# Shorter pauses in a hand-woven instruction order, and weights that are loaded in four blocks of partitions

## The chip, the cores and the metric

The kernel runs on one core of one Trainium2 chip. The metric is the device time in microseconds (us) of one execution; lower is better. A core has five engines that each work through their own instructions in order and meet only through semaphores: TensorE (PE), VectorE (DVE), ScalarE (ACT), GpSimd (POOL) and SyncE (SP), which here only issues transfers.

## What is computed

The input is x, 16 images of 32 channels of 128 x 128 float32. Four layers follow each other; each normalises x over pairs of channels, computes something from it, and adds the result to x (in the last layer it is x times something).

```python
x = x + L0(gn(x))   # layer 0: a row-wise LSTM along the diagonals, 128 steps
x = x + L1(gn(x))   # layer 1: quantised 3x3 "adder" convolution, -sum |patch - w|
x = x + L2(gn(x))   # layer 2: Hartley transform, 32 x 32 modes mixed, transform back
x = x + L3(gn(x))   # layer 3: five edge operators, normalised over a group of images,
                    #   conv1, pool, conv2, pool, conv3, pool, conv4,
                    #   then three times (deconv 2x2, conv 3x3); times the layer's input
```

Layer 3 normalises each edge operator over an image, so its statistics need a whole image before its first convolution can begin. Layers 2 and 3 treat the images in four groups of four; a group needs layer 1 finished for its own four images and nothing of the other groups.

## The kernel before

**Stages.** `stage0` computes layer 0. `rest` computes the other three. Layer 1 is the class `Differences`: for each image and each half of it (64 rows) it makes 72 arrays of 128 x 8192 float16, max(q - w, 0), one for each tap and block of four output channels, and TensorE adds them up over the input channels. An array (a "tap step" below) is made either by VectorE (line 758, tile `d_dve`, three buffers) or by ScalarE (line 755, tile `d_act`, two buffers); 16 matmuls (line 645) add up one of them. Layers 2 and 3 are the class `After`; for one group `g` it runs in this order:

| step | lines | what it does |
|---|---|---|
| `forward` | 1028-1156 | loads x (`xh`, 1050), transforms columns (1116), turns (1131), transforms rows (1088), stores the modes (1098) |
| `modes`, `add` | 1158-1186 | reads the modes back in two orders (`xs`, `xw`, 1168), combines them on VectorE (1175, 1182) |
| `mixing` | 1193-1228 | mixes channels mode by mode (1203), weights `mix` by 1 MB loads (1190), stores `z` |
| `back` | 1230-1333 | transforms back (1267, 1312), adds to x on VectorE and stores (`take_out`, 1290-1296), new statistics |
| `statistics` | 1376-1488 | Gram matrices of the image rows on TensorE (1403), then the five operators' statistics on VectorE (1463) from tables `gm` |
| `first_layers` | 1504-1542 | folds the operators into conv1's weights (1530, 1532) from tables `v` that GpSimd loads (1517), then conv1 |
| `conv1` | 1662-1775 | borders (1693), then 25 taps of 16 matmuls for each of 8 chunks of 16 rows (1721), pooled and spread into `y1` (1645, 1656, 1659) |
| `small_layers` | 1544-1630 | conv2 to conv4 (1568), two upsamplings (902, 927), weights by `replicated` (819) |
| `last` | 1777-1868 | the third upsampling (902), times x (1850, 1813, 1823), result stored |

**What sets the order.** The order on every engine is decided when the program is built. `Differences.run` writes out its own tap steps and, between two of them, calls `weave.advance`, which puts in as much of `After.work` (a generator) as a small planner finds room for. The planner (`Weave`) keeps an estimated time for each engine: 2.36 us for a tap step on VectorE, 7.15 us on ScalarE, 1 us for its sums on TensorE. The generator yields a positive number after it has emitted that much TensorE work, and a negative one for a pause: `yield -4.0` means that the generator gives nothing more until 4 us have passed on the planner's clock. A pause is no instruction. It only decides how many tap steps, or how many instructions of another group, are emitted ahead of the next instruction, so that this one finds its data when its engine comes to it. `weave.later(24.0, step)` does the same for a single deferred step. Leftover time in which TensorE would be idle during layer 1 is filled with matmuls by zero (`keep_busy`, line 675).

Groups 0 to 2 are woven into layer 1 in this way. What is left of them when layer 1 ends, and group 3, whose images are finished only then, are emitted by `drain`: it takes in turn from the two generators whichever stands earlier on its own planner clock, with all pauses multiplied by 1.5, and by 1 once one of the two is exhausted. Below, "layer 1" is the stretch up to the last tap step, and "the tail" is what comes after it.

**Loads.** SP issues nearly all transfers, in program order. `by_rows` issues one transfer for each block of 32 partitions:

```python
def by_rows(nc, tile, dram, store=False):
    for j in range(4):
        part = tile[32 * j : 32 * j + 32]
        rows = bass.AP(dram.tensor, dram.offset + j * dram.ap[0][0], [list(v) for v in dram.ap[1:]])
```

`replicated` loads small convolution weights four times over, once for each block of 32 partitions, by a single transfer whose source has an outermost dimension of four with step zero. It is called 19 times: seven times in `prepare`, and once for conv2 and twice for conv3 and conv4 in each of the four groups.

Of the kernel before, what the change touches and what calls it, by code (L numbers as in the profile page):

```python
# [815 lines left out]
def replicated(nc, pool, src, n, name):  # L816

    wr = pool.tile([128, n, 32], F32, name=name)
    nc.sync.dma_start(wr, bass.AP(src.tensor, src.offset, [[0, 4], [n * 32, 32], [1, n * 32]]))
    return wr  # L820


# [133 lines left out]
class After:  # L956
# [71 lines left out]
    def forward(self, g):  # L1028

        nc, tc, cst, d, weave = self.nc, self.tc, self.cst, self.d, self.weave  # L1030
        x2, xm_d, z_d = d["x2"], d["xm"], d["z"]
        ahead = self.buffers["t_x"]
        with self.pool("t_m") as mp:
# [9 lines left out]
            with self.pool("t_t") as tp, ExitStack() as rows:  # L1043
# [21 lines left out]
                p = self.acc()  # L1065
# [83 lines left out]
                rows.close()  # L1149
                wp = rows.enter_context(self.pool("t_w", self.buffers["t_w"]))  # L1150
                wt = [self.weights(wp, i) for i in range(self.buffers["t_w"])]
                yield -36.0
                for n in range(8):
                    while steps[n]:
                        weave.done(steps[n])
# [2 lines left out]
    def modes(self, g, b, pool, xs, steps):  # L1158

        nc, weave, xm_d = self.nc, self.weave, self.d["xm"]  # L1160
        xw = pool.tile([128, 16, 32], F32, name="xw", bufs=self.buffers["xw"])
        first = xm_d.offset + (4 * g + b) * 32768
        for half in range(2):
            part = slice(64 * half, 64 * half + 64)
            for dst, at in ((xs[part, 4 * half + b], 512 * half), (xw[part], 512 - 512 * half)):
                rows = bass.AP(xm_d.tensor, first + at, [[1024, 32], [1, 512]])
                for r in range(2):
                    nc.sync.dma_start(dst[32 * r : 32 * r + 32].rearrange("p k y -> p (k y)"), rows)

        def add():  # L1170
            for half in range(2):
                part = slice(64 * half, 64 * half + 64)
                x, sign = xs[part, 4 * half + b], self.cst["sign"][part]

                nc.vector.tensor_copy(xw[part, 0, :], x[:, 0, :])
                for dst, neg in (
                    (x[:, 1:, 1:], xw[part, :0:-1, :0:-1]),
                    (x[:, 1:, 0], xw[part, :0:-1, 0]),
                    (x[:, 0, 1:], xw[part, 0, :0:-1]),
                    (x[:, 0, 0:1], xw[part, 0, 0:1]),  # L1180
                ):
                    nc.vector.scalar_tensor_tensor(dst, neg, sign, dst, ALU.mult, ALU.add)
            weave.dve += 2.4
            steps[2 * b + 1] = None

        steps[2 * b + 1] = weave.later(24.0, add)

    def weights(self, pool, i):
        w = pool.tile([128, 4, 16, C], F32, name="mix")
# [3 lines left out]
    def mixing(self, g, xs, wp, wt):  # L1193


        nc, weave, z_d = self.nc, self.weave, self.d["z"]
        zp = [self.acc() for _ in range(2)]
        zv = [z.rearrange("p (y k b) -> p y k b", k=4, b=8) for z in zp]
        for ky in range(M1):
            w = wt[ky // 4]  # L1200
            for k in [4 * j + i for i in range(4) for j in range(4)]:
                j = k // 4
                nc.tensor.matmul(  # L1203
                    zv[ky // 16][32 * j : 32 * j + 32, ky % 16, k % 4, :],
                    w[:, ky % 4, k, :],
                    xs[:, :, k, ky],
                    start=True,
                    stop=True,
                )
            if ky % 4 == 3 and len(wt) < M1 // 4:  # L1210
                wt.append(self.weights(wp, len(wt)))
            yield 1.0
            if ky % 4 == 3 and 8 < ky < M1 - 1 and not weave.draining:
                yield -5.0
        yield SUMMED
        zs = wp.tile([128, 2, 4, 4, 32], F32, name="zs", bufs=1)
        for half in range(2):
            for y in range(2):
                dst = zs[:, half, :, :, 16 * y : 16 * y + 16].rearrange("p b k y -> p y k b")
                nc.vector.tensor_copy(dst, zv[y][:, :, :, 4 * half : 4 * half + 4])  # L1220
        weave.dve += 2.0
        yield -2.5
        for half in range(2):
            for j in range(4):
                first = z_d.offset + 4 * g * 32768 + 512 * half + 128 * j
                dst = bass.AP(z_d.tensor, first, [[1024, 32], [32768, 4], [1, 128]])
                nc.sync.dma_start(dst, zs[32 * j : 32 * j + 32, half].rearrange("p b k y -> p b (k y)"))
        yield -4.0

    def back(self, g, load):  # L1230

# [5 lines left out]
        with self.pool("t_z") as zp_, self.pool("t_r", ahead) as rp:  # L1237
# [68 lines left out]
            for n in range(16):  # L1306
                s, half = n // 2, n % 2
                pf = [self.acc() for _ in range(2)]
                for i in range(4):
                    for r in range(2):  # L1310
                        part = slice(64 * half + 32 * r, 64 * half + 32 * r + 32)
                        nc.tensor.matmul(  # L1312
                            pf[r][:, W * i : W * i + W],
                            o1[part, 4 * s + i].rearrange("p b o -> p (b o)"),
                            cst["cas_t"][part, :],
                            start=True,
                            stop=True,
                        )
                yield 0.8
                if previous:  # L1320
                    yield -4.5
                    take_out(*previous)
                previous = n, pf
            yield SUMMED
# [51 lines left out]
    def statistics(self, g, pool, frames, sides, out, tables):  # L1376
# [14 lines left out]
            nc.gpsimd.dma_start(gm[k], self.a["gram"][:, k])  # L1391
        f = pool.tile([128, 24], F32, name="es_f")
        ends = (slice(2, 4), slice(W, W + 2))
        yield -14.0
        gram = [self.acc() for _ in range(4)]

        def products(xp, l, rows, width, at, start, stop):
# [51 lines left out]
                ready[ch + ahead, half] = weave.later(2.0, following)  # L1449
            yield -1.0  # L1450
        tables()
        yield -3.0

        for k, s in enumerate((1, 0, 3, 2)):
            nc.vector.tensor_reduce(f[:, 4 + k : 5 + k], sides[:, 2 : H + 2, s], AX.X, ALU.add)
# [4 lines left out]
        for k in range(5):  # L1460
            for blk in range(4):
                w = pool.tile([128, GRAM], F32, name="es_w", bufs=1)
                nc.vector.tensor_tensor_reduce(  # L1463
                    w, gram[blk][:, :GRAM], gm[k], 1.0, 0.0, ALU.mult, ALU.add, accum_out=red[:, blk, k : k + 1]
                )
                weave.dve += 0.7
                if blk % 2:
                    yield -1.0
            if len(gm) < 5:
                gm.append(pool.tile([128, GRAM], F32, name="gm", bufs=tables_ahead))  # L1470
                nc.gpsimd.dma_start(gm[-1], self.a["gram"][:, len(gm) - 1])
        yield -2.0
        p = self.acc()
# [30 lines left out]
    def first_layers(self, g, fp, frames, y2):  # L1504
        nc, tc, weave = self.nc, self.tc, self.weave
        sides = fp.tile([128, H + 4, 4], F32, name="sides")
        ops = fp.tile([128, 2, 5], F32, name="ops")
        wf = fp.tile([128, 90, 32], F32, name="wf")
        b1 = fp.tile([128, 4], F32, name="b1")
        with self.pool("e_v", self.buffers["e_v"]) as pool:  # L1510
            v = []

            def table():

                k, half = len(v) // 2, len(v) % 2
                v.append(pool.tile([128, 45, 32], F32, name="v"))
                nc.gpsimd.dma_start(
                    v[-1].rearrange("p t o -> p (t o)"), self.d["fold"][k, :, 1440 * half : 1440 * half + 1440]
                )

            with self.pool("e_s") as es:
                yield from self.statistics(g, es, frames, sides, ops, lambda: [table() for _ in range(self.buffers["e_v"])])
            yield -0.5
            for n in range(10):
                k, half = n // 2, n % 2
                for part, i in (((0, 81 - 45), 0), ((81 - 45, 45), 1)) if half else (((0, 45), 0),):
                    s = ops[:, i, k : k + 1]
                    to, t = wf[:, 45 * half + part[0] : 45 * half + part[1]], v[n][:, part[0] : part[1]]
                    if k == 0:
                        nc.vector.tensor_scalar(to, t, s, None, ALU.mult)  # L1530
                    else:
                        nc.vector.scalar_tensor_tensor(to, t, s, to, ALU.mult, ALU.add)
                    weave.dve += 0.1 + 0.033 * (part[1] - part[0])
                if len(v) < 10:
                    table()
                yield -2.0
        with self.pool("e_y1") as y1p:
            y1 = self.padded(y1p, 64, "y1")
            self.wc = {"conv2": replicated(nc, y1p, self.a["conv2"], 9, "w_conv2")}
            yield from self.conv1(g, y1p, frames, y1, sides, wf, b1)  # L1540
            with self.pool("e_c2") as cp:
                yield from self.small_layers(cp, None, y1, y2)

    def small_layers(self, cp, rp, y1, y2):
# [3 lines left out]
        if not y1:  # L1548
# [2 lines left out]
            up5, up6 = self.up5.loaded(cp), self.up6.loaded(cp)  # L1551
            y3, y4, y5 = (self.padded(cp, n, f"y{i}") for n, i in ((16, 3), (16, 4), (32, 5)))
            self.y6 = y6 = self.padded(rp, 64, "y6")
            yield -12.0

        def conv(src, n, name, evict):
            rows = min(n // 4, 512 // n)
# [45 lines left out]
        def upsampled(src, n, up, dst):  # L1603

            rows = min(n, 512 // n)
            for r in range(0, n, rows):
# [3 lines left out]
                for blk in range(4):  # L1610
# [8 lines left out]
                        up.bias,  # L1619
                        nc.vector if n == 16 or blk % 2 else nc.scalar,  # L1620
                    )
                yield -2.0 if n == 16 else -8.0

        if y1:
            yield from conv(y1, 64, "conv2", pool_into(y2, 64, 1))
# [404 lines left out]
```

## Time and profile before

| | us |
|---|---|
| median of 3 runs | 6794.93 (6793.73 to 6800.52) |
| the profiled execution, its own time | 6791.52 |
| its span, first to last instruction | 6789.7 |
| layer 1, first to last tap step on VectorE | 689 to 5594 |
| the tail | 5592 to 6790 |
| of the tail: TensorE busy | 940.6 |

The profiled execution's time is 1.8 us above its span and 3.4 us below the median. In the profile, a row of a group view gives line, engine, operation, what it writes and reads, its count, the time in which the engine was busy with it, the mean of one, and the idle time of the engine ahead of it with what ended that idle time. A row of the window view gives, for each engine, busy time and number of instructions in a stretch, then TensorE's granted clock, and the busy share and rate of the transfers. Float32 matmuls stand in the profile as two records each, so one conv1 tap of 16 matmuls is 32 records.

When layer 1 ends in this execution, group 2 is in its `statistics`: 5555 to 5685 us. Its conv1 runs from 5773 to 6122 and its `last` from 6302 to 6506. Group 3 starts at the end of layer 1: transforms from 5653, mixing from 5740, back from 5818, statistics from 6053, conv1 from 6253 to 6593, the end at 6790.

### The profile page before, as it was taken

Reading aid. Unit: us, or ns where it says so; the run is one execution under the profiler, and the core shown is the slowest. Engines: PE = TensorE matmul, PEld = TensorE weight load, DVE = VectorE, ACT = ScalarE, POOL = GpSimd, SP = SyncE. Lnnn points to the kernel's source line nnn. Section 1 sums busy time; section 2 is a strip of 40 time slices with the busy share of each in tenths; the row PEclk is TensorE's granted clock in tenths of the full one; section 3 lists DMA queues with packets and bytes.
Section 4 is the critical chain, followed back from the end, with each engine's and each line's share of the span. In section 5 each row is a group of like instructions: output and inputs, shape, how many; then the busy total and the mean of one; then the engine's idle time right before and its main releaser. Section 6 shows DMA issues by size and latency. Waiting matters only on the chain. (4 is left out here: it accounts for less than half of the span.)

```text
span 6789.7 us, 271989 instructions
## 1 busy us (share of the span) xinstructions
PE 5402.1 (80%) x127580; PEld 2816.8 (41%) x127580; DVE 5640.5 (83%) x6946; ACT 5537.1 (82%) x3419; POOL 90.9 (1%) x83
## 2 busy tenths in 40 slices
PE   3697777787777879997877788999877774897896
PEld 3575333333343433333334343333333343454564
DVE  7898999999999999989999999999999993224223
ACT  3898999999999999999999999999999991132222
POOL 0000000000000010000000000000000000000000
PEclk9998999999999989998989899999889996997997
DMA  7553312213343431312353443222264246342414
GB/s 316 201 189 126 77 49 63 60 30 71 80 127 108 113 109 46 85 44 59 86 152 92 145 117 79 56 57 51 61 139 120 66 135 194 99 149 72 92 42 104
DMA packets 381685, 689.12 MB, mean 101 GB/s; under 512 B 68048, under 2 KB 234448, under 8 KB 369680
## 3 DMA queue, kind: packets, MB, share of 16 engines
q1 hardware_dynamic: 373088, 637.30, 34.2%
q0 software_dynamic: 7040, 33.80, 1.5%
q8 instruction: 998, 16.35, 1.0%
q14 instruction: 127, 1.04, 0.1%
q10 hardware_dynamic: 432, 0.64, 0.0%
HBM read 507.28 MB, written 164.32 MB: 99 GB/s over the span
## 5 line engine op out<-in xcount | busy, mean ns | idle before, releaser
L755 ACT ACTIVATE d_act<-q,neg 128x8192 f16<-128x8192 f16 (+1 forms) x622 | 4404.3, 7148 | 138.0 <-PE acc L645 117.2
L758 DVE TENSOR_SCALAR d_dve<-q,qw 128x8192 f16<-128x8192 f16 (+1 forms) x1682 | 3878.9, 2363 | 163.5 <-PE acc L645 143.3
L645 PE MATMUL acc<-d_dve,sel 128*32 128x512 f16 x26912 | 1864.5, 400 | 475.4 <-DVE d_dve L758 412.2
L645 PEld LDWEIGHTS <-sel 128*32 128x32 f16 x36864 | 1014.3, 100 | 2122.4 <-issue 1455.1
L1721 PE MATMUL acc<-xp,wf 32*32 32x512 f32 x25600 | 1040.4, 616 | 57.4 <-issue 53.3
L645 PE MATMUL acc<-d_act,sel 128*32 128x512 f16 x9952 | 716.4, 408 | 329.6 <-ACT d_act L755 310.0
L1721 PEld LDWEIGHTS acc<-xp,wf 32*32 32x32 f32 x25600 | 416.1, 104 | 429.0 <-issue 345.8
L1659 ACT ACTIVATE y<-pooled,b 32x128 f32<-32x128 f32 x488 | 195.1, 400 | 389.1 <-DVE pooled L1645 382.4
L675 PE MATMUL acc<-q,zero 128*32 128x512 f16 x7088 | 509.2, 399 | 0.0
L902 PE MATMUL acc<-y,u_conv 32*32 32x256 f32 (+1 forms) x9728 | 373.8, 472 | 90.8 <-issue 63.7
L221 PE MATMUL pg<-h,wb 64*64 64x20 f32 (+15 forms) x8192 | 340.1, 303 | 61.5 <-DVE h L249 35.3
L235 ACT ACTIVATE gt<-pg,bias 128x20 f32<-128x20 f32 (+15 forms) x1024 | 332.5, 384 | 42.3 <-PE pg L221 40.4
L1362 ACT ACTIVATE xp<-xp,shift,stats 128x1280 f32<-128x1280 f32 (+1 forms) x128 | 182.6, 1434 | 185.8 <-DMA xp<-x_d 170.6
L221 PEld LDWEIGHTS pg<-h,wb 64*64 64x64 f32 x8192 | 250.1, 149 | 136.9 <-DVE h L249 82.5
L675 PEld LDWEIGHTS <-zero 128*32 128x32 f16 x7088 | 214.7, 101 | 195.7 <-issue 40.2
L1850 DVE TENSOR_SCALAR s<-acc,l_ms,l_one 128x512 f32<-128x512 f32 x128 | 102.1, 821 | 202.8 <-PE acc L902 202.8
L902 PEld LDWEIGHTS acc<-y,u_conv 32*32 32x32 f32 x9728 | 177.0, 111 | 216.4 <-issue 164.2
L1823 ACT ACTIVATE xr<-xr,l_ms 128x1024 f32<-128x1024 f32 x64 | 70.0, 1141 | 222.8 <-DVE xr L1813 222.8
L1403 PE MATMUL acc<-xp 32*64 32x204 f32 (+3 forms) x8576 | 238.6, 344 | 16.1 <-issue 15.6
L1403 PEld LDWEIGHTS acc<-xp 32*64 32x64 f32 (+1 forms) x8576 | 168.2, 135 | 108.9 <-issue 100.4
L221 PE MATMUL pg<-xn,wb 64*64 64x2 f32 (+63 forms) x4096 | 184.1, 289 | 28.6 <-issue 18.6
L1568 PE MATMUL acc<-y,w_conv 32*32 32x512 f32 (+2 forms) x4608 | 162.5, 497 | 28.4 <-issue 16.5
(218 smaller groups left out, 3711.9 us busy)
## 6 DMA issues: line engine op xcount, KB each, us to landing
xp<-x_d SPq DMA_DIRECT2D x112, 640.0 KB
q<-q_d SPq DMA_DIRECT2D x128, 536.2 KB
xr<-x_d SPq DMA_DIRECT2D x128, 512.0 KB
x_in<-in_x_dram SPq DMA_DIRECT2D x16, 2048.0 KB
xn<-in_xs_dram SPq DMA_DIRECT2D x64, 512.0 KB
res<-in_x_dram SPq DMA_DIRECT2D x64, 512.0 KB
x_d<-res SPq DMA_DIRECT2D x64, 512.0 KB
xq<-x_d SPq DMA_DIRECT2D x256, 128.0 KB
```

The costliest lines, as they stand in the source:

```text
L221: nc.tensor.matmul(bank[c][q][64 * pair : 64 * pair + 64, :, :width], wb[half, 4 * kind + KIND[q]].rearrange("p b o -> p (b o)"), v[half], ...
L235: nc.scalar.activation(gt[:, q, :, :n], bank[c][q][:, :, :n], AF.Tanh if q == G else AF.Sigmoid, bias=bias[:, KIND[q] : KIND[q] + 1],)
L645: self.nc.tensor.matmul(acc[k][32 * j : 32 * j + 32, :], self.sel16[:, i // 9, :], d[:, row : row + 4, c : c + W], start=first, stop=last,)
L675: self.nc.tensor.matmul(acc[k][32 * j : 32 * j + 32, :], self.zero, q[:, :4, :W], start=False, stop=False)
L755: nc.scalar.activation(dst, src, AF.Relu, bias=self.neg[:, i : i + 1])
L758: nc.vector.tensor_scalar(dst, src, self.qw[:, i : i + 1], 0.0, ALU.subtract, ALU.max)
L902: nc.tensor.matmul(acc[blk][32 * j : 32 * j + 32, o : o + rows * n], t[part, 4 * par + tap, :], src[part, top : top + rows, left : left + ...
L1362: nc.scalar.activation(v, v, AF.Identity, bias=self.shift3, scale=self.stats3[:, 1])
L1403: nc.tensor.matmul(gram[blk][j : j + width, at : at + n], xp[part, l, 2 + j : 2 + j + width], xp[part, rows, j : j + width + 4], start=sta ...
L1568: nc.tensor.matmul(acc[blk][32 * j : 32 * j + 32, : rows * n], wc[name][part, tap, :], src[part, at : at + rows, kw : kw + n], start=tap == 0,
L1659: nc.scalar.activation(d, s, AF.Identity, bias=bj)
L1721: nc.tensor.matmul(acc[blk][32 * j : 32 * j + 32, :], tap_of("all", tap)[rows], xp[rows, 4 * j + kh : 4 * j + kh + 4, kw : kw + W], start= ...
```

## The change

Ten pauses and one deferral of `After` become shorter, and `replicated` loads through `by_rows`, by four transfers in place of one. The tap steps, the planner's costs, the buffers and the arithmetic are as before. Pauses by place: before mixing 36 to 21, before `add` 24 to 14, within mixing 5 to 2.5, after storing `z` 4 to 1.5, before each `take_out` 4.5 to 3.2 (16 a group), before `statistics` 14 to 9, after its loop 3 to 1, between the operators' statistics 1 to 0.4, between folds 2 to 1.2, before conv3 12 to 7, after a round of the second upsampling 8 to 4.5.

```diff
 def replicated(nc, pool, src, n, name):
     wr = pool.tile([128, n, 32], F32, name=name)
-    nc.sync.dma_start(wr, bass.AP(src.tensor, src.offset, [[0, 4], [n * 32, 32], [1, n * 32]]))
+    whole = bass.AP(src.tensor, src.offset, [[0, 4], [n * 32, 32], [1, n * 32]])
+    by_rows(nc, wr.rearrange("p t o -> p (t o)"), whole)
     return wr
...
@@ forward
-                yield -36.0
+                yield -21.0
...
@@ modes
-        steps[2 * b + 1] = weave.later(24.0, add)
+        steps[2 * b + 1] = weave.later(14.0, add)
...
@@ mixing
-                yield -5.0
+                yield -2.5
...
-        yield -4.0
+        yield -1.5
...
@@ back
                 if previous:
-                    yield -4.5
+                    yield -3.2
                     take_out(*previous)
...
@@ statistics
-        yield -14.0
+        yield -9.0
...
         tables()
-        yield -3.0
+        yield -1.0
...
                 if blk % 2:
-                    yield -1.0
+                    yield -0.4
...
@@ first_layers
                     table()
-                yield -2.0
+                yield -1.2
...
@@ small_layers
-            yield -12.0
+            yield -7.0
...
-                yield -2.0 if n == 16 else -8.0
+                yield -2.0 if n == 16 else -4.5
```

## The prediction

> **What bounds the kernel now.** I read the page first, its shares and its forty slices.
>
> ```profile
> PE 5402.1 (80%) x127580; PEld 2816.8 (41%) x127580; DVE 5640.5 (83%) x6946; ACT 5537.1 (82%) x3419; POOL 90.9 (1%) x83
> ...
> PE   3697777787777879997877788999877774897896
> DVE  7898999999999999989999999999999993224223
> ACT  3898999999999999999999999999999991132222
> ```
>
> The shares of 80 to 83% average over two regimes. In slices 5 to 33 VectorE and ScalarE are full and TensorE is not: layer 1. In the last seven slices TensorE is the busy one: the tail. The window view, cut at layer 1's end and at group 3's steps, says how much room each stretch has.
>
> ```profile
> 689.00:5592.00 4903.00, 3998.74 (x85394) 1851.80 (x85394) 4685.09 (x3858) 4753.48 (x1230) 74.12 (x45) 0.93 0.33 85
> 5592.00:5740.00 148.00, 73.71 (x1762) 53.94 (x1754) 68.23 (x222) 27.14 (x43) 5.32 (x11) 0.72 0.74 219
> 5740.00:5818.00 78.00, 58.24 (x2702) 34.96 (x2704) 5.88 (x28) 0.00 (x0) 0.21 (x1) 0.76 0.17 45
> 5818.00:6006.00 188.00, 167.96 (x4942) 95.23 (x4929) 62.19 (x131) 48.45 (x110) 0.00 (x0) 0.98 0.50 149
> 6006.00:6166.00 160.00, 151.73 (x4744) 83.45 (x4713) 30.50 (x133) 61.62 (x127) 6.47 (x14) 0.99 0.38 113
> 6166.00:6253.00 87.00, 57.78 (x1845) 35.42 (x1842) 63.50 (x180) 7.72 (x13) 2.14 (x4) 0.64 0.19 59
> 6253.00:6593.00 340.00, 302.92 (x9573) 204.45 (x9585) 80.98 (x182) 76.20 (x145) 0.21 (x1) 0.95 0.30 69
> 6593.00:6790.00 197.00, 128.25 (x4385) 84.65 (x4353) 82.38 (x168) 48.38 (x80) 0.00 (x0) 0.78 0.43 96
> ```
>
> The columns are stretch, length, then busy time on PE, PEld, DVE, ACT and POOL. In layer 1 (first row) ScalarE is busy 97% and VectorE 96%: what is woven in there costs their time. In the tail TensorE works 941 of 1198 us. The largest hole is the first 148 us, half idle. The group view of the tail shows two of its causes.
>
> ```profile
> L1203 PE MATMUL acc<-xs,mix 128*32 128x8 f32 x1024 | 16.3, 192 | 33.4 <-DVE xs L1182 28.2 <-issue 5.2
> ...
> L1066 PE MATMUL acc<-diag,cw 32*128 32x256 f32 x2 | 1.2, 710 | 15.2 <-DVE diag L1061 15.2
> ```
>
> Group 3's mixing waits 28 us for its modes; before that its scales wait 15 us on a VectorE that is held by group 2's statistics. So the question is how much more of group 2 is done when the tail begins, what that costs in layer 1, and whether the tail gets shorter by it.
>
> **What the skill says.** The Trainium skill, Perfetto Trace Analysis, section Optimization Strategy: where the most-contended engine changes over time, interleaving the regimes may pay. The rows above agree that there are two regimes. DMA: Bandwidth & Descriptors, section Rules for kernel authors: a leading zero-stride dimension of c copies confines a transfer to at most c of the 16 engines. That is the old form of `replicated`; the trace has no landing times for SP's transfers, and nobody is shown waiting for line 819, so it neither agrees nor disagrees. The same page, Anatomy of one DMA: a semaphore wait is served by the issuing sequencer ahead of dispatch, so a transfer that waits holds SP's queue; here SP spent 1075 us in 56 waits at line 338 for `qt`.
>
> **Where the work moves.** The order of both programs' instructions on each engine can be compared. At the last tap step the changed program stands further: 784 of the 1072 instructions of group 2's Gram matrices (line 1403), its 352 border matmuls (1693), 192 matmuls of conv1 (12 of 200 taps), 20 of its operators' statistics pairs (40 records of line 1463) and all 12 of its accumulating folds (1532) have left the tail. Group 2 is about 100 us of the tail's work ahead, from pauses of two and a half groups. Groups 1 and 2 begin `forward` 19 and 59 VectorE tap steps earlier (956 for 975, 1456 for 1515).
>
> **Cost in layer 1.** Means from the group rows. VectorE gains 40 x 0.337 + 12 x 1.215 + 3 x 0.716 + 22 x 0.173 (line 1433) and small ones, in all 42.4 us. ScalarE gains 15 normalisations (1362) of 1.434 and their edges, 28.4 us. The planner also makes 4 tap steps on ScalarE rather than VectorE (1682 to 1678, 622 to 626): -4 x 2.363 and +4 x 7.148. Sum: VectorE +33.0, ScalarE +57.0. Its last tap step ended at 5590, VectorE's at 5594, so layer 1 ends at 5590 + 57 = 5647: +53. TensorE's extra work, 45 us of Gram matrices and 14 of conv1, takes the place of 23 rounds of 16 zero matmuls (24 us) and of idle time. Some of it will hold up sums:
>
> ```profile
> DVE d_dve L758 <- PE acc L645: 143.3, 97, 7.1
> ...
> ACT d_act L755 <- PE acc L645: 117.2, 51, 8.3
> ```
>
> These two waits (us in total, times, longest) grow in proportion to woven work if all goes as before, some 5% of 117, but part of it is paid by zero matmuls: +2. I take +55.
>
> **Cost of the shorter pauses themselves.** A pause is no instruction; if too short, the next instruction waits at the head of an in-order engine with tap steps (DVE) or their sums (PE) behind it.
> - `add`, 24 to 14: in layer 1 it started 10.8 to 24.5 us after the last of its loads was issued, never waiting. 10 us less leaves 0.8 to 14.5. In the tail two of them waited 4.8 us and ran 0.2 and 0.8 us after that issue, so a landing takes little over that. Cost 0 to 4 us per group; I take 0. Mixing, 36 to 21, follows the last `add` anyway.
> - Mixing's weights: a 1 MB load was issued some 30 us before use (5206.6 for 5237.1); 2.5 us less for every four rows of three buffers leaves over 20. Nothing.
> - Folds, 2 to 1.2: before, one or two between tap steps; now three to seven. A table buffer comes back after three folds, and a table lands 6.0 us after its issue on POOL's queue (720 KB). Three folds of 1.2 to 1.7 us and one tap step are about 7, so where seven folds stand together VectorE waits some 3 to 4 us: up to 10 us over three groups. Gram tables: 1.8 us once before, up to 3 a group. VectorE has 24 us less to add than ScalarE, which covers these; without that cover they would cost 15.
> - `take_out`: 16 per group, still mostly two tap steps apart; `xr` was reloaded 24 us ahead. Conv3's weights were issued 23 us ahead, now 18. The rest defer nothing that was late. Nothing.
> - `replicated`: 19 issues of 0.57 us become 76 of 0.42: 21 us more of SP, spread over the program, with nobody waiting; between -1 and +1 us each if on the path. I take 0. Behind them on SP stand the composed weights (issued 6594, used 6636) and the frames; 2 us do not reach either.
>
> **Gain in the tail.** A conv1 tap takes 1.17 us (1897 records in an unbroken 69.4 us of the chain). For each stretch, group 3's own work plus what the changed order puts beside it:
> 1. To mixing (148): Gram matrices give way to 63 taps, 71 us, with 23 of transforms; the last 30 us still wait for the modes. 138.
> 2. Mixing (78): 14 + 50 taps (56) and issue gaps: 77.
> 3. Back (188): 75 taps in place of 112, some conv2: work 132 for 162, with the 26 us of waits as before: 160.
> 4. Statistics (160): 53 + conv2 to conv4 (27) + the third stage's first rounds (19), no conv1: 99, and 20 of waits: 119.
> 5. Tables (87): a chain of transfers and VectorE, 86.
> 6. Conv1 (340): 200 taps, and 624 in place of 1088 matmuls of group 2's last upsampling: 300.
> 7. Alone (197): unchanged; pauses no longer order anything. 197.
>
> Sum 1077 for 1198: -121; I take -120. Check by work: TensorE loses 75 us, VectorE's hold-ups ahead of it (15 + 10 + 8) go, issue gaps lose 15: -123.
>
> **Sum.** +55 - 120 = -65. The profiled execution's 6791.5 becomes 6726.5; the median stood 3.4 above it: 6730.
>
> **Rivals.**
> - *Group 3's chain is the bound.* For it: stretches 1 and 5 have TensorE idle 50 and 34%. If stretches 1 to 5 keep their lengths and only the sixth falls by 40, layer 1's +55 and 15 us of uncovered table waits are paid for a gain of 40: 6795 + 30 = 6825. It decides as soon as the tail gives back less than 70. Against it: stretches 3 and 4 have TensorE at 89 and 95%. Chance 0.13.
> - *TensorE fills every hole.* Work 866, issue gaps 142, and 34 of waits at the end: 1042, -156; with +52 in layer 1, 6690. Against it: the changed order puts only eight taps before the mixing, where 30 us are idle. Chance 0.14.
> - *The lead is lost in waits of layer 1.* Early instructions stall it by 60 us, 20 a group, over my bound: 6795. Chance 0.09.
> - *The change does not do what it says*: excluded by the order, 784 instructions moved.
>
> **Chances.** Forecast 0.64 (6700 to 6780). A measurement of this kernel can tell 0.2% (14 us) from no change. Faster: 0.64 + 0.14 = 0.78; same 0.09; slower 0.13. The range 6680 to 6800 leaves out the first rival and the fast edge of the second.
>
> **What would show it.** The last tap step near 5647; group 3's conv1 of 300 us; the last stretch of 197; table waits on VectorE under 15 us in all. I am wrong if the waits of tap steps for TensorE rise by tens of us, or if group 3's mixing still begins 148 us after layer 1 with its statistics no earlier.

## The result and the profile after

| | before | changed | ratio, 95% interval |
|---|---|---|---|
| median, us | 6797.73 (4 runs) | 6739.66 (4 runs) | 0.9917, 0.9900 to 0.9934 |
| the profiled execution, us | 6791.52 | 6751.99 | |
| its span, us | 6789.7 | 6750.2 | |

The change makes the kernel 58 us faster; 65 were forecast, and 6739.66 lies 10 us above the forecast of 6730 and inside its range. The profiled execution of the changed kernel is the slowest of its four and stands 12 us above their median, that of before 6 below its own: the two profiles differ by 39.5 us, so stretches compared between them understate the gain by some 18.

The page of the changed kernel: the same two regimes, with the change of regime one slice later (column 35 of the forty).

```profile
PE 5402.1 (80%) x127212; PEld 2825.9 (42%) x127212; DVE 5639.1 (84%) x6966; ACT 5552.5 (82%) x3399; POOL 85.9 (1%) x83
...
PE   3798777788777879997877779998787788887795
...
DVE  7898999999999999999999998899999996144223
ACT  3898999999999999999999999999999996122112
```

Its window view, cut at the end of layer 1 and at group 3's steps (columns as in the forecast):

```profile
689.00:5662.00 4973.00, 4066.16 (x87694) 1881.00 (x87686) 4711.68 (x3972) 4800.11 (x1275) 74.50 (x56) 0.92 0.33 87
5662.00:5784.00 122.00, 103.39 (x2383) 48.97 (x2366) 42.06 (x136) 23.21 (x46) 0.00 (x0) 0.93 0.61 176
5784.00:5866.00 82.00, 73.98 (x2624) 42.38 (x2624) 9.44 (x41) 19.56 (x44) 0.21 (x1) 0.92 0.36 99
5866.00:6031.00 165.00, 142.99 (x4149) 84.68 (x4136) 59.79 (x123) 32.27 (x77) 0.21 (x1) 0.90 0.42 127
6031.00:6182.00 151.00, 113.63 (x3609) 78.13 (x3610) 57.34 (x196) 49.41 (x85) 6.24 (x13) 0.84 0.57 150
6182.00:6266.00 84.00, 49.68 (x1924) 32.62 (x1926) 49.37 (x113) 8.05 (x10) 2.13 (x4) 0.59 0.40 102
6266.00:6553.00 287.00, 258.41 (x8224) 197.11 (x8207) 62.68 (x166) 55.45 (x109) 0.21 (x1) 0.96 0.22 51
6553.00:6750.00 197.00, 124.14 (x4386) 80.68 (x4379) 82.61 (x170) 48.35 (x80) 0.00 (x0) 0.77 0.43 96
```

Layer 1 is longer and the tail is shorter. The first row is 70 us longer than before's. Its busy time grew by 27 us on VectorE and 47 on ScalarE; its idle time (length less busy time) grew from 218 to 261 us on VectorE and from 150 to 173 on ScalarE. The tail's first stretch fell from 148 to 122 us, with TensorE now 85% busy in it, and conv1's from 340 to 287. Counted to the end of the last tap step, layer 1 ends at 5658.5 for 5592.0, and began 2.7 us earlier: +69. The tail is 1091.7 us for 1197.7: -106. Layer 1 differs by up to 17 us between the profiles of runs (below) with the same compute order in it: 4903 us before, 4920 in e1 and 4904 in e4; 4972 in the changed kernel and 4962 in e3. The group view of the tail says what became of the two holes:

```profile
L1204 PE MATMUL acc<-xs,mix 128*32 128x8 f32 x1024 | 14.1, 188 | 18.3 <-DVE xs L1183 10.9 <-issue 7.5
...
L1067 PE MATMUL acc<-diag,cw 32*128 32x256 f32 x2 | 0.7, 426 | 0.0
```

The wait for the scales (15.2 us) is gone, that for the modes fell from 28.2 to 10.9. Line numbers from 820 on are one higher than before; those below are of the changed kernel where its lines are shown.

### The profile page after: what moved, and what is told of

The parts are those of the page before. It is cut to its first block, busy times and chain, and to the rows that moved or that the text cites. A ratio compares the mean times of both kernels' runs of the same rounds, so it can differ in the third digit from the quotient of the medians.

```text
span 6750.2 us, 271326 instructions
## 1 busy us (share of the span) xinstructions
PE 5402.1 (80%) x127212; PEld 2825.9 (42%) x127212; DVE 5639.1 (84%) x6966; ACT 5552.5 (82%) x3399; POOL 85.9 (1%) x83
## 4 chain that ended last, share of the span: by engine, by line
PE 21%; issue 14%; DVE 8%; ACT 6%; DMA 2%; SPq 1%; POOL 0%; DVEq 0%; ACTq 0%; POOLq 0%
PE acc L1722 8%; ACT d_act L755 5%; PE acc L645 5%; DVE d_dve L758 4%; PE acc L903 2%; PE acc L1404 1%; PE acc L1569 1%; DVE y L1657 1%; ACT xp L1363 0%; DMA mix<-in_mix_dram 0%; PE acc L928 0%; DMA v<-fold_d 0%; PE acc L1694 0%; DMA xm_d<-xm 0%; PE acc L1313 0%
## 5 line engine op out<-in xcount | busy, mean ns | idle before, releaser
L1722 PE MATMUL acc<-xp,wf 32*32 32x512 f32 x25600 | 1012.0, 623 | 33.0 <-issue 28.3
L1722 PEld LDWEIGHTS acc<-xp,wf 32*32 32x32 f32 x25600 | 431.8, 105 | 387.3 <-issue 307.4
L675 PE MATMUL acc<-q,zero 128*32 128x512 f16 x6720 | 481.9, 399 | 0.0
L903 PE MATMUL acc<-y,u_conv 32*32 32x256 f32 (+1 forms) x9728 | 356.5, 485 | 95.7 <-issue 53.0
L675 PEld LDWEIGHTS <-zero 128*32 128x32 f16 x6720 | 200.2, 101 | 185.6 <-issue 38.3
L1758 DVE TENSOR_TENSOR acc<-acc,cut 128x4 f32<-128x4 f32 x256 | 35.2, 164 | 232.5 <-PE acc L1722 230.1
```

The source lines that it names most:

```text
L675: self.nc.tensor.matmul(acc[k][32 * j : 32 * j + 32, :], self.zero, q[:, :4, :W], start=False, stop=False)
L903: nc.tensor.matmul(acc[blk][32 * j : 32 * j + 32, o : o + rows * n], t[part, 4 * par + tap, :], src[part, top : top + rows, left : left + ...
L1722: nc.tensor.matmul(acc[blk][32 * j : 32 * j + 32, :], tap_of("all", tap)[rows], xp[rows, 4 * j + kh : 4 * j + kh + 4, kw : kw + W], start= ...
```

## The experiments

All times are medians of four runs and more, beside runs of the kernel before on the same chip; the ratio is to those. The theory is that of the forecast, "the lead": the gain is group 2's work that leaves the tail. Its rivals are the loads and the order inside the tail; later runs ask for the price of single pauses.

**e1: the loads alone.** The kernel before, with `replicated` as changed.

```diff
-    nc.sync.dma_start(wr, bass.AP(src.tensor, src.offset, [[0, 4], [n * 32, 32], [1, n * 32]]))
+    whole = bass.AP(src.tensor, src.offset, [[0, 4], [n * 32, 32], [1, n * 32]])
+    by_rows(nc, wr.rearrange("p t o -> p (t o)"), whole)
```

> The kernel before with the four-block weight loads alone, all pauses as before. Lead theory (the gain is work of group 2 that leaves the tail for layer 1): no waiter stood behind these loads, so no change, within 0.2% of before (6784 to 6811). Rival, the loads: if they were what helped, some 6740.

Measured 6791.25, ratio 0.9993 (0.9985 to 1.0001): no difference that can be told. The loads of small weights are not the gain.

**e3 and e4: the short pauses in one regime only.** In e3 they hold while work is woven into layer 1, in e4 only in the tail; every pause of the change is written like this one (e4 with the two numbers exchanged):

```diff
-                yield -21.0
+                yield -36.0 if self.weave.draining else -21.0
```

> The changed kernel with the short pauses only while work is woven into layer 1; in the tail every pause has its old length. Lead theory: the state at the last tap step is that of the changed kernel (784 Gram matmuls and 12 conv1 taps fewer in the tail), so most of the gain stays, 6735 to 6760. Rival, the order in the tail (shorter pauses there interleave groups 2 and 3 better): the lead is paid for and nothing is got back, 6797 or more.

> The changed kernel with the short pauses only in the tail; while work is woven into layer 1 every pause has its old length. Lead theory: layer 1 ends as before and the tail has all of its work; mixing may start 10 to 15 us earlier, so 6780 to 6797. Rival, the order in the tail: the whole gain, about 6740.

Measured: e3 6735.94, ratio 0.9912 (0.9898 to 0.9926), the whole gain; e4 6809.56, ratio 1.0014 (1.0006 to 1.0022), none, and slightly slower than before where a small gain was expected. The gain comes from the pauses inside layer 1. In the tail they bring nothing: e3's tail, with the old pauses, is 1086 us long, the changed kernel's 1092. Without the lead they cost something there: e4's tail is 1216 us long, for 1198 before and 1200 in e1.

**e5: the same pauses without the lead.** One pause of 200 us before group 0 uses the lead up again.

```diff
-                yield -8.0
+                yield -200.0 if g == 0 else -8.0
```

> The changed kernel, all pauses short, but with one pause of 200 us before group 0, so that the lead is gone: 1824 Gram matmuls are left in the tail, for 1856 before and 1072 in the changed kernel. Lead theory: layer 1 is as short as before, the tail as long: 6780 to 6800. Rival, the order in the tail, or denser weaving as such: about 6740.

Measured 6867.6, ratio 1.0100 (1.0087 to 1.0113). The gain is gone, as the lead theory says, but the kernel is 70 us slower than before, which no theory had. Its tail is 1213 us, 16 more than before and like e4's 1216. Its layer 1 is 4962 us for 4903, although VectorE and ScalarE do almost the same work in it (4682 for 4685 us, 4757 for 4753): the 59 us are waiting. So the short pauses have a price of their own in layer 1, or the shifted start has; the next runs look for its place.

**e7: part of the pauses.** Only the four around the mixing stay short; all others are as before.

```diff
-                    yield -3.2
+                    yield -4.5
...
-        yield -9.0
+        yield -14.0
...
-        yield -1.0
+        yield -3.0
...
-                    yield -0.4
+                    yield -1.0
...
-                yield -1.2
+                yield -2.0
...
-            yield -7.0
+            yield -12.0
...
-                yield -2.0 if n == 16 else -4.5
+                yield -2.0 if n == 16 else -8.0
```

> The changed kernel with short pauses only around the mixing (before it, before its combining step, within it, after storing its result); all others as before. Its tail has 1328 Gram matmuls left, for 1856 before and 1072 in the changed kernel, and all borders. Lead theory: a smaller lead, a smaller gain, about half: 6755 to 6780. Rival, one of the other pauses carries the gain: 6797; or the mixing's pauses carry all of it: 6740.

Measured 6756.79, ratio 0.9941 (0.9927 to 0.9955): a lead of 528 Gram matmuls gives 39 us, that of the changed kernel (784, the borders and 12 taps) gives 58. More lead, more gain; the four pauses around the mixing carry about two thirds of it.

**e6 and e9: the pause between folds.** One stretch of layer 1 in which idle time grew runs from the first fold to the first conv1 tap. Here it is in the window view for groups 0 and 1 before:

```profile
2447.00:2520.00 73.00, 52.65 (x1428) 26.17 (x1427) 71.40 (x53) 72.79 (x25) 14.83 (x8) 0.91 0.40 111
4076.00:4148.00 72.00, 55.14 (x1458) 26.12 (x1471) 71.50 (x52) 68.15 (x25) 14.82 (x8) 0.88 0.32 92
```

and for groups 0 to 2 after, with the folds of group 0 alone in the last row:

```profile
2404.00:2468.00 64.00, 34.34 (x1000) 17.79 (x999) 50.59 (x46) 52.86 (x21) 8.69 (x8) 0.65 0.56 152
4015.00:4077.00 62.00, 32.38 (x948) 16.33 (x951) 47.44 (x46) 50.66 (x20) 7.09 (x8) 0.64 0.57 157
5572.00:5637.00 65.00, 42.30 (x1236) 19.75 (x1244) 56.92 (x44) 57.20 (x22) 5.51 (x8) 0.79 0.31 101
2404.00:2432.00 28.00, 11.54 (x120) 4.85 (x119) 26.54 (x25) 27.88 (x9) 8.69 (x8) 0.69 0.60 190
```

Before, VectorE and ScalarE are nearly full (71 and 68 to 73 of 72 us); after, each stands idle for 8 to 15 us, and TensorE's clock is 0.64 to 0.79 for 0.88 and 0.91. The stretch is shorter by some 9 us, but only 20, 18 and 25 tap steps begin in it instead of 33. As layer 1 makes one in 2.13 us on average (4903 us for 2304), the missing steps are worth more than the 9 us. e9 shortens the pause between folds alone, in the kernel before with the new loads. e6 puts it back in the changed kernel, and with it, which its expectation does not say, the pause between the operators' statistics:

```diff
-                    yield -0.4
+                    yield -1.0
...
-                yield -1.2
+                yield -2.0
```

> The changed kernel with the pause between folds back at 2 us, all else as changed. Theory of the folds: at 1.2 us three to seven folds stand between two tap steps, TensorE has nothing to add up, its granted clock falls to 0.6 to 0.8 there, and the border matmuls and sums behind it run slow while tap steps wait; with 2 us the clock stays near 0.9 and layer 1 loses 15 to 35 us: 6705 to 6725. Rival: the waits there come from how tap steps and borders happen to meet, or the pause is free: 6735 to 6745, like the changed kernel.

> The kernel before (with the four-block weight loads) and only the pause between folds at 1.2 us. Its tail has 1888 Gram matmuls left, no lead. Theory of the folds: the two groups woven in pay 10 to 15 us each: 6810 to 6825. Rival, the pause is free or useful: 6790 to 6800.

Measured: e6 6717.3, ratio 0.9886 (0.9872 to 0.9900); e9 6822.35, ratio 1.0044 (1.0032 to 1.0057). Both as the theory of the folds has it in size. e6 is faster than both kernels. The comparison with the changed kernel is clear of noise: e10 below, which has the changed order and was measured beside e6, took 6735.94 at its fastest, and e6 6724.67 at its slowest. e6's three stretches:

```profile
2407.00:2482.00 75.00, 48.93 (x1324) 24.69 (x1327) 74.80 (x59) 72.59 (x25) 13.37 (x8) 0.89 0.46 130
3986.00:4064.00 78.00, 52.31 (x1312) 25.38 (x1320) 68.10 (x53) 70.89 (x23) 14.93 (x8) 0.80 0.46 125
5550.00:5620.00 70.00, 52.12 (x1461) 25.07 (x1465) 69.74 (x48) 69.71 (x23) 14.83 (x8) 0.95 0.26 79
```

They take 223 us for 97 tap steps, where the changed kernel takes 191 for 63: 34 steps, worth 72 us, for 32 us. These 40 us are an upper estimate: layer 1 is 4942 us in e6 and 4972 in the changed kernel, 30 apart, and the medians are 22 apart; the tails are alike (1094 and 1092). By group, e6 gives 11, 16 and 5 us for 14, 12 and 8 steps, which gains 19, 10 and 12 us by the same price.

The second pause of e6 has little part in this. On VectorE the two kernels have the same order up to the first fold of group 0, and the statistics ahead of the folds last 29, 27 and 25 us in both; only in group 1 one tap step more stands between them in e6. It was not tried alone.

For e9 the place is wrong. Its folds in groups 0 and 1 stand between tap steps exactly as the changed kernel's do in group 1, but its layer 1 is only 7 us longer than before, less than runs with the same order differ. 22 of its 27 us lie in the tail (1220 us), where the folds of groups 2 and 3 stand. So this one pause is enough for the longer tails of e4 and e5. Why it costs that much there is not settled.

Part of e5's surplus lies in the same stretches. In groups 0 and 1 they take 60 and 64 us there, and 25 and 15 tap steps begin in them, where before 33 and 33 do in 73 and 72 us: 26 steps, worth 55 us, for 21 us. By this price that is 34 of its 59 us; the rest was not traced.

**e10: is it the clock?** The changed kernel with four matmuls after each woven fold, into a spare bank that nobody reads (one more line, not shown, names the constants that they read).

```diff
+                if not weave.draining:
+                    p = self.ps.tile([128, 512], F32, name="acc")
+                    for j in range(4):
+                        nc.tensor.matmul(
+                            p[32 * j : 32 * j + 32],
+                            self.cst["ident128"][:, :32],
+                            self.cst["all"][:, :512],
+                            start=True,
+                            stop=True,
+                        )
                 yield -1.2
```

> The changed kernel, and after each fold in layer 1 four matmuls into a spare bank whose result nobody reads (10 a group, about 1 us each); order on VectorE and ScalarE as in the changed kernel. If the fallen clock makes the folds dear: the clock in folds and borders rises above 0.8, waits fall, 6715 to 6735. If it is VectorE's burst itself (tap steps and tables that come late), or the sums that are late for other reasons: 6740 to 6750 with the clock up.

Measured 6740.48, ratio 0.9919 (0.9906 to 0.9933): no gain. The two halves of group 0's stretch, folds and then borders, in e10:

```profile
2409.00:2434.00 25.00, 16.44 (x172) 5.74 (x161) 22.28 (x19) 23.27 (x6) 8.68 (x8) 0.86 0.64 207
2434.00:2475.00 41.00, 25.24 (x904) 13.83 (x903) 27.50 (x28) 28.95 (x15) 0.00 (x0) 0.67 0.48 111
```

The changed kernel's borders of group 0, for comparison:

```profile
2432.00:2468.00 36.00, 22.80 (x892) 12.94 (x883) 24.05 (x22) 24.98 (x13) 0.00 (x0) 0.62 0.53 123
```

The clock in the folds is up at 0.86 from 0.69, and VectorE stands idle in the borders as before (13 of 41 us, for 12 of 36). A higher clock in the folds does not help. In the borders the clock rose only from 0.62 to 0.67, so this run does not tell what a higher one there would do.

**e11 to e14: the loads of q.** In the changed kernel the four loads of the next half's q (2.1 MB) are issued at 2443 and 4055 us, on the border matmuls of groups 0 and 1; before, they fell outside. In group 0 the order on SP shows how: before, q's loads (2414 us) stand ahead of those of conv2's weights (2484); in the changed kernel they stand behind them, and SP waits 50 us for the end of the folds before it issues these weights (2428). e11 and e13 issue q's loads later in the changed kernel, e12 and e14 in e6, both of whose pauses they have.

```diff
-                    if i == 8 and (b, half) != (B - 1, 1):
+                    if i == 24 and (b, half) != (B - 1, 1):
```

(48 in place of 24 for e13 and e14.)

> The changed kernel; only the four loads of the next q (2.1 MB) are issued at tap step 24 of a half instead of 8, so that they no longer fall on the border matmuls of groups 0 and 1. Order on the compute engines as in the changed kernel. If TensorE's own instruction supply suffers from those loads there: issue gaps in the borders of groups 0 and 1 fall from 12 to about 4 us, tap steps wait less, layer 1 shrinks by 15 to 25 us: 6715 to 6730. Rival, the packed folds are what makes those stretches slow, wherever q is loaded: 6735 to 6745.

> The changed kernel with the fold pause back at 2 us and the loads of q at tap step 24. If the folds and the loads of q are two costs: 6695 to 6712. If the fold pause of 2 us helped only because it moved the borders away from the loads of q: no better than either alone, 6713 to 6730.

> The changed kernel with the four loads of the next q at tap step 48 of a half instead of 8 (step 24 moved them by only 8 us in group 0 and left them on the borders). Compute order as in the changed kernel. If the loads of q on top of the borders are what slows those stretches: transfer share there under 0.3, issue gaps about 4 instead of 12 us, waits of VectorE and ScalarE there under 5 us each in groups 0 and 1. The time may still be 6730 to 6760, since step 24 cost 17 us elsewhere. Rival, packed folds alone: the borders stay at 25 us and more with gaps of 10 or more although the transfers are gone.

> The changed kernel with the fold pause back at 2 us and q loaded at tap step 48. If moving q costs elsewhere what it saves at the borders: 6717 to 6740, no better than the fold pause alone. If the fold pause and the loads of q are separate gains: under 6710.

| | time | ratio to before |
|---|---|---|
| e11, q at 24 | 6757.16 | 0.9948 (0.9936 to 0.9960) |
| e12, q at 24 and e6's pauses | 6736.95 | 0.9914 (0.9900 to 0.9927) |
| e13, q at 48 | 6745.69 | 0.9925 (0.9911 to 0.9940) |
| e14, q at 48 and e6's pauses | 6732.14 | 0.9905 (0.9887 to 0.9923) |

e11 tests nothing at the borders: SP was already behind by the wait named above (49 us there), and the loads moved only from 2443 to 2451 us, still on top of them. e13 moved them off. The waits in group 0's borders in the changed kernel (us in total, times, longest):

```profile
PE acc L1694 <- issue: 12.5, 4, 7.3
DVE d_dve L758 <- PE acc L645: 12.0, 4, 7.1
ACT d_act L755 <- PE acc L645: 10.9, 2, 6.6
```

and in e13:

```profile
PE acc L1694 <- issue: 5.9, 4, 2.2
...
DVE d_dve L758 <- PE acc L645: 4.2, 3, 3.3
```

TensorE's gaps halve, VectorE waits a third, and the stretches of groups 0 and 1 shrink by 8 to 9 us each with the same compute order in them:

```profile
2406.00:2461.00 55.00, 33.28 (x996) 17.64 (x999) 49.39 (x45) 54.14 (x21) 8.68 (x8) 0.63 0.46 137
4014.00:4068.00 54.00, 29.93 (x968) 15.43 (x983) 46.57 (x44) 47.06 (x20) 7.09 (x8) 0.72 0.46 140
```

e12 shows the reverse: there the load fell on group 0's borders, which e6 had kept free, and the gaps at line 1694 went from 3.8 us to 8.3 with the compute order of layer 1 unchanged:

```profile
PE acc L1694 <- issue: 3.8, 3, 1.7
...
PE acc L1694 <- issue: 8.3, 5, 5.4
```

The other groups agree. Of the 36 border stretches of layer 1 in the fourteen profiles, 12 have loads of q issued during them or up to 2 us ahead: their gaps are 8.3 to 14.1 us each. The 24 others have 1.1 to 6.2.

So the loads of q on the borders cost about 16 us in these two stretches of the changed kernel. The packing of the folds costs something without them: in group 1 the loads lie on the borders in e6 as well as in the changed kernel, in group 2 in neither, and there e6 still gains 10 and 12 us by the price above. As a change of the kernel the move is no gain: e13's layer 1 is 4969 us for 4972, and the times of e11 to e14 are no better than those without it, so the loads cost elsewhere what they save here.

**What holds TensorE in these gaps.** The profile puts them down to "issue", but its records of the transfers have a pattern. Queue q8, called "instruction", moves 995 packets of 16 KB in the changed kernel, one for every 256 of TensorE's 254,424 records; I take them for TensorE's own instructions. All 119 of these gaps in the border stretches of the fourteen profiles (over 0.15 us, 215 us in total) end 1.2 to 1.7 us after such a packet has landed, although one comes only every 3.4 to 4 us there in the kernel before. In the tail, too, 131 of 155 us of TensorE's issue gaps before, and 157 of 158 after, end 1.1 to 1.8 us after one. The longest gap of group 0 in the changed kernel, and the same place in e13:

```profile
2457.32 0.81 PE L1694 MATMUL acc<-sides,wf 32*32 32x32 f32 x55 [7.32 <-issue]
...
2452.93 0.74 PE L1694 MATMUL acc<-sides,wf 32*32 32x32 f32 x55 [0.60 <-issue]
```

The two gaps ahead of it are alike in both kernels (2.1 and 2.8 us, 2.1 and 2.2). The packet that ends the long one began at 2454.5 us and had landed at 2455.9; the packet before it began 10.4 us earlier. In e13 these two begin 5.7 us apart. The queues from 2445.5 to 2454 us (packets, MB, share of the 16 transfer engines), in the changed kernel, with no q8 at all, and in e13:

```profile
q1 hardware_dynamic: 161, 1.85, 103.9%
...
q1 hardware_dynamic: 263, 0.69, 28.1%
q8 instruction: 1, 0.02, 1.0%
```

By these times TensorE ran out of instructions, and longest while the loads of q filled the transfer engines. No run changed the instruction transfers themselves, so this is read from times and not tested.

## Why the prediction was right, point by point

The mechanism was right: a lead is paid for in layer 1 and comes back, larger, in the tail. The net number was closer than its two parts: in the profiles layer 1 cost 14 us more than forecast and the tail gave 14 us less, and the medians are 18 us kinder than this pair of profiles.

- **What moves.** Right: e3, e5 and e7 show that the lead carries the gain, e1 and e4 that loads and order in the tail don't.
- **The tail, -120.** The profiles say -106. By stretch, forecast and measured: to mixing 138 and 122, mixing 77 and 82, back 160 and 165, statistics 119 and 151, tables 86 and 84, conv1 300 and 287, alone 197 and 197. Group 3's wait for its modes shrank more than I allowed (10.9 us for 30), and the "20 of waits" in the statistics were too few: TensorE is idle for 37 us there, 25 of them issue gaps at line 1404. The errors of -16, +32 and -13 nearly cancel, which is luck. (63 and 50 taps at 1.17 us are 74 and 59 us, not 71 and 56; it matters little.)
- **Layer 1, +55.** It was +69 in the profile. The step was that ScalarE, with 57 us more, sets the end, and that VectorE's 24 us of slack cover the table waits. Its start was misread: ScalarE's last tap step before began at 5576.2 and took 7.1 us, so it ended at 5583, not 5590, and VectorE's at 5592, not 5594. ScalarE's busy time grew by 47 us rather than 57 (13 normalisations moved, not 15). e6 shows what the moved work costs with the folds spread as before: +39, between the 26 us by which VectorE's busy time grew there and ScalarE's 47. The other 30 us go with the short pauses at folds and statistics, which I had costed at 0 to 10 under cover. This is the term that was mis-sized.
- **Table waits.** VectorE waited 7.0 us, 7 times, for the tables, as estimated (up to 10). What I missed was that packed folds leave TensorE without sums and the tap steps behind them waiting, several times that price:

```profile
DVE d_dve L758 <- PE acc L645: 167.5, 111, 7.1
...
DVE wf L1533 <- DMA v<-fold_d: 7.0, 7, 2.1
...
DVE xw L1176 <- DMA xw<-xm_d: 2.3, 1, 2.3
```

- **Waits of tap steps for sums, "+2".** Mis-sized: VectorE's rose from 143 to 168 us, ScalarE's from 117 to 127, 34 us together. The prediction had named a rise "by tens of us" as a sign of being wrong; it came true, and the gain stood all the same. In e6 they are back at 139 and 106.
- **`add`.** In layer 1 the least margin left was forecast at 0.8 us; one instance of twelve waited, 2.3 us. Right there. In the tail it was not free: all eight copies of group 3 waited for their modes, 27.7 us in total where three waited 11.1 before. The mixing behind them began earlier even so.
- **`replicated`.** Forecast at 0; e1 gives -6 us with an interval that includes 0.
- **Rivals.** TensorE did not fill every hole, group 3's chain was not the bound, and the lead was not lost in waits of layer 1. A part of that last rival was real: 22 us go with the two pauses of e6 (6739.66 for 6717.3).

## What to carry to other kernels

Where instructions of one stage are woven into another by a fixed order, a shorter pause pays by how much work has left the under-used stage at the end; compare the orders of both programs there, then test it by using the lead up again. Look at the stretch behind each pause, in main steps per microsecond, and not only at the wait of its own instruction: the pause between folds looked nearly free, and with its neighbour it cost 22 us. The count of steps gives an upper estimate (40 us here). Where a stretch is bound by one busy engine, like the tail here, shorter pauses brought nothing, and without the lead they cost 16 to 22 us.

## What was not expected of the hardware

- The gaps of TensorE in a stretch of small matmuls (32 x 32 x 32, 0.22 us each) went with the load on the transfers: 12.5 us at line 1694 while 2.1 MB of q were loaded on top, 5.9 once they were moved (e13), and over all profiles 8.3 to 14.1 us with such loads and 1.1 to 6.2 without. All 119 of them end 1.2 to 1.7 us after a 16 KB packet of the instruction queue has landed.
- Raising TensorE's granted clock in the folds from 0.69 to 0.86 by matmuls that nobody reads changed the kernel's time by less than could be told (6740.48 for 6739.66).
